# Two transformer layers on one core: layer 1's reciprocals per head and repeated by ScalarE, two pieces of layer 0 issued later

## The chip, the core and the metric

The kernel runs on one core of a Trainium2 chip. The core has TensorE (PE, matrix products; PEld is its weight load), VectorE (DVE), ScalarE (ACT), GpSimd (POOL) and SyncE (SP, here only an issuer of DMA transfers). Each engine works through its own queue in order and waits on semaphores for the others. The metric is the device time of one execution in microseconds; lower is better.

## The reference

Input is x of 2 sequences with 1024 tokens of 128 channels, all in float32. Two pre-norm layers are applied, each an attention and a mixture of experts, each added to x:

```python
x = x + _L0_attn_ref(_layernorm(x), ...)   # 16 heads of 64, with biases, no mask
x = x + _L0_ffn_ref(_layernorm(x), ...)    # 8 gated experts, top 2
x = x + _L1_attn_ref(_layernorm(x), ...)   # 16 heads of 8 plus 32 rotary dims, causal
x = x + _L1_ffn_ref(_layernorm(x), ...)    # a shared MLP and 8 experts, top 2
```

What matters for the change is in the two attentions. In layer 0, with s = 1/sqrt(64):

```python
q = z @ wq @ fcq_w + fcq_b;  k = z @ wk @ fck_w + fck_b
attn = softmax(q @ k.T * s);  out = attn @ v
```

In layer 1 each head has only 8 value channels, so a query tile's output is 16 heads x 8 channels = 128 rows, and each row is divided by its head's softmax sum.

## The kernel before

Tokens stand in tiles of 128. PSUM is split by three pools: ps_s (2 wide buffers for scores), ps_t (3 banks for transposes and everything small) and ps_a (1 accumulator). Inside `tc.manual_schedule` the instructions of TensorE, VectorE and ScalarE (in layer 1 GpSimd too) stand in the order in which the program issues them; elsewhere a scheduler places them. L404 and L415 are issued outside such a block, and the trace shows where they were put on VectorE: L404 between the statistics and L135, L415 between the normalisations.

*Start.* x is loaded by SP, then the three bias columns (L401, L404's input among them), while ScalarE issues the weight loads and GpSimd those of the router and the experts. L404 scales the query bias by s. `latents(0)` (L420) is the first layer norm (statistics L128 and L129, square root on ScalarE L134, reciprocal on VectorE L135, normalisation L153, transposes L147) and the projections to latents (L432, L433, L437). `project_qk` (L475) makes queries and keys of one pair of heads; ScalarE adds the biases (L488).

*Layer 0.* The loop at L600 runs over units (sequence b, pair of heads pr, query tile qt), 128 units. Three units are in flight: unit i gets scores (L501), row maximum (L510, VectorE) and exponentials (L520, ScalarE); unit i−1 gets its probabilities transposed (`fill`, L551) and moved out (`evict`, L557, one half by ScalarE, one by VectorE); unit i−2 gets its values (L568). When a pair is complete, at qt = 1 of the next pair, `reciprocals` (L523) inverts its softmax sums, 128x16, and `scale` (L528) transposes them on TensorE (L532), copies them out by ScalarE (L534), sends them by SP to DRAM (L538) and back, spread over partitions (L540, two transfers), and GpSimd multiplies the pair's output (L542). `project_qk` of the following pair stands in the units qt = 1 and 5. Side work fills other units: the layer norm of sequence 1 and the output weights while b = 0, `project_out` of sequence 0 at (1, 1), the router of sequence 0 from (1, 2). Layer 0's experts follow.

*Layer 1.* The loop at L1201 has the same shape, with causal lengths: scores L1078, masked maximum L1086, exponentials L1108, transposes L1120 with evictions L1126, values L1160. Units with qt < 4 are "short" and are issued two at a time. After the last unit of a query tile, `reciprocals` (L1129) inverts the softmax sums with each head's sum already repeated over its 8 channels: 128x128, and once more the first 64 columns (L1134, L1135). In the next unit `spread` (L1138) transposes the result (four matmuls, L1143), ScalarE copies it (L1145), and VectorE multiplies the tile's output (L1167). Sixteen query tiles end this way.

Of the kernel before, what the change touches and what calls it, by code (L numbers as in the profile page):

```python
# [11 lines left out]
F32 = mybir.dt.float32  # L12
# [3 lines left out]
ALU = mybir.AluOpType  # L16
# [3 lines left out]
P = 128  # L20
# [3 lines left out]
NT = T // P  # L24
# [5 lines left out]
H0, D0 = 16, 64  # L30
H1, D1, DR = 16, 8, 32
# [15 lines left out]
def bc(ap, shape):  # L47
    return ap.to_broadcast(list(shape))
# [3 lines left out]
def two_layers(ctx, tc, a, out):  # L52
    nc = tc.nc
# [9 lines left out]
    small = ctx.enter_context(tc.tile_pool(name="small", bufs=4))  # L63
# [4 lines left out]
    def bank():  # L68
        return psum["t"].tile([P, QB], F32, tag="t", name="ps_t")

    def acc_bank():
        return psum["a"].tile([P, QB], F32, tag="a", name="ps_a")

    def load(pool, name, shape, src, eng):
        t = pool.tile(list(shape), F32, tag=name, name=name)
        eng.dma_start(out=t if len(src.shape) == 2 else t.rearrange("p (a b) -> p a b", b=src.shape[-1])
                      if len(shape) == 2 else t, in_=src)
        return t
# [155 lines left out]
    def route0(b, pool, tag, bufs, got, gap):  # L234
        yield from layernorm_steps(b, pool, got, bufs, tag, gap=gap)
        yield
        yield from gates0(b, got)
# [149 lines left out]
    with ExitStack() as st:  # L387
# [11 lines left out]
        bias = {}  # L399
# [1 line left out]
            bias[k] = load(w0, f"b{k}", [P, NP], a[f"fc{k}"][D0:D0 + 1, :].rearrange("o (j p) -> p (o j)", p=P),  # L401
                           nc.sync)
        scaled_bq = w0.tile([P, NP], F32, tag="scaled_bq", name="scaled_bq")
        nc.vector.tensor_scalar(scaled_bq, bias["q"], 1.0 / math.sqrt(D0), None, ALU.mult)  # L404
        fco = load(w0, "fco", [P, NP, C], a["fco_w"].rearrange("(j p) c -> p j c", p=P), nc.scalar)
        fco_b = load(w0, "fco_b", [1, C], a["fco_b"], nc.scalar)

# [12 lines left out]
        def latents(b):  # L420

            got = []
            yield from layernorm_steps(b, a0, got, first=(b == 0))
            lnT = got[0]
            zqk = a0.tile([P, T], F32, tag="zqk", name="zqk", bufs=2)
            zv = a0.tile([P, NT, D0], F32, tag="zv", name="zv", bufs=2)
            lat[b] = zqk, zv
            for n in range(NQB):
                yield
                cols = slice(n * QB, (n + 1) * QB)  # L430
                ps = bank()
                nc.tensor.matmul(ps, wqk, lnT[:, cols], start=True, stop=True)  # L432
                nc.vector.tensor_copy(zqk[:, cols], ps)  # L433
            yield
            ps = bank()
            for t in range(NT):
                nc.tensor.matmul(ps[:, t * D0:(t + 1) * D0], lnT[:, t * P:(t + 1) * P], wv, start=True, stop=True)  # L437
            nc.scalar.copy(zv.rearrange("p t d -> p (t d)"), ps)
# [36 lines left out]
        def project_qk(b, pr, n):  # L475

            if n == 0:
                qk = a0.tile([P, 2, T], F32, tag="qk", name="qk", bufs=2)
                pairs[b, pr] = qk
            qk = pairs[b, pr]  # L480
            z, cols = lat[b][0], slice(n * QB, (n + 1) * QB)

            got = [acc_bank(), bank()]
            for h in range(2):
                rows = slice(h * D0, (h + 1) * D0)
                nc.tensor.matmul(got[h], fcqk[rows, pr * P:(pr + 1) * P], z[rows, cols], start=True, stop=True)  # L486
            for h, (scale, add) in enumerate(((1.0 / math.sqrt(D0), scaled_bq), (1.0, bias["k"]))):
                nc.scalar.activation(qk[:, h, cols], got[h], AF.Identity, bias=add[:, pr:pr + 1], scale=scale)  # L488
# [3 lines left out]
        probs, probsT, sums, recips, accs, aoTs = {}, {}, {}, {}, {}, {}  # L492
# [30 lines left out]
        def reciprocals(key):  # L523
            rs = small.tile([P, 2, NT], F32, tag="rs0", name="rs0", bufs=2)
            nc.vector.reciprocal(rs, sums.pop(key))
            return rs

        def scale(key, rs):  # L528

            b, pr = key  # L530
            ps = bank()
            nc.tensor.transpose(ps[:2 * NT, :P], rs.rearrange("p h t -> p (h t)"), ident)  # L532
            rows = small.tile([2 * NT, P], F32, tag="rsT0", name="rsT0", bufs=2)
            nc.scalar.copy(rows, ps[:2 * NT, :P])  # L534

            r = a0.tile([P, T], F32, tag="recip", name="recip", bufs=2)
            flat = dr.tile([2, T], F32, tag="flat", name="flat")
            nc.sync.dma_start(out=flat.rearrange("h (t p) -> (h t) p", p=P), in_=rows)  # L538
            for h in range(2):
                nc.sync.dma_start(out=r[h * D0:(h + 1) * D0, :], in_=bc(flat[h:h + 1, :], [D0, T]))  # L540
            o = aoTs[b][:, pr, :]
            nc.gpsimd.tensor_tensor(o, o, r, ALU.mult)  # L542
# [12 lines left out]
        def evict(i, h, ps, copy):  # L555
            for r in range(2):
                copy(probsT[i][h][:, :, r * 64:(r + 1) * 64], ps[r].rearrange("p (j q) -> p j q", q=64))  # L557
# [30 lines left out]
        with tc.manual_schedule(engines={ET.PE, ET.DVE, ET.Activation}):  # L588
            lat = {}
            for _ in latents(0):  # L590
                pass
            project_qk(0, 0, 0)
            project_qk(0, 0, 1)
            wout = w0.tile([P, NP, C], F32, tag="wout", name="wout")
            extra = [latents(1), output_weights()]
            routing = route0(0, f0w, "lnT", 1, routed0[0], 1)
            temp = [lambda: a0.tile([P, T], F32, tag="pT", name="h0", bufs=6)[:, :QB],
                    lambda: a0.tile([P, T], F32, tag="p", name="o0", bufs=4)[:, :QB]]
            experts = experts0(0, routed0[0], temp)
            for i in range(N + 3):  # L600
                s = scores(i) if i < N else None
                if 1 <= i <= N:
                    probsT[i - 1] = [a0.tile([P, NT, P], F32, tag="pT", name="pT", bufs=6) for _ in range(2)]
                    evict(i - 1, 0, fill(i - 1, 0), nc.scalar.copy)
                if i < N:
                    exponentials(i, [maximum(s[0]), maximum(s[1])])
                done = units[i - 2][:2] if i >= NT and i % NT == 1 else None
                if done:
                    rs = reciprocals(done)
                if 2 <= i <= N + 1:  # L610
                    values(i - 2)
                if 1 <= i <= N:
                    evict(i - 1, 1, fill(i - 1, 1), nc.vector.tensor_copy)
                    del probs[i - 1]
                if i >= N:
                    if i == N + 1:
                        scale(done, rs)
                        for t0 in (0, TPB):
                            project_out(NB - 1, t0, TPB, range(NP - 1))
                    experts(i < N + 2)  # L620
                    continue
                b, pr, qt = units[i]
                after = (b, pr + 1) if pr + 1 < NP else (b + 1, 0)
                if after[0] < NB and qt in (1, 5):
                    project_qk(*after, qt // TPB)
                if done:
                    scale(done, rs)
                if b == 0 and pr and qt not in (1, 5) and extra:
                    if next(extra[0], N) == N:
                        extra.pop(0)  # L630
                        if not extra:
                            obias = output_bias()
                            for bb in range(NB):
                                nc.gpsimd.tensor_tensor(xs[bb], xs[bb], bc(obias.unsqueeze(1), [P, NT, C]), ALU.add)
                if (b, pr) == (1, 1):
                    project_out(0, qt, 1, range(NP))
                if b == 1 and pr > 1 and qt not in (1, 5):
                    next(routing, None)
            for t0 in (0, TPB):
                project_out(NB - 1, t0, TPB, [NP - 1])  # L640
# [415 lines left out]
    with ExitStack():  # L1056
        units = [(b, qt, pr) for b in range(NB) for qt in range(NT) for pr in range(8)]
        N = len(units)
        probs, probsT, sums, recips, accs, outs = {}, {}, {}, {}, {}, {}
# [69 lines left out]
        def reciprocals(key):  # L1129


            full = small.tile([P, H1 + H1 // 2, D1], F32, tag="rsw1", name="rsw1", bufs=1)
            total = sums.pop(key)
            nc.vector.reciprocal(full[:, :H1, :], bc(total.unsqueeze(2), [P, H1, D1]))  # L1134
            nc.vector.reciprocal(full[:, H1:, :], bc(total[:, :H1 // 2].unsqueeze(2), [P, H1 // 2, D1]))  # L1135
            return full.rearrange("p h d -> p (h d)")

        def spread(key, full):  # L1138
# [40 lines left out]
        with tc.manual_schedule(engines={ET.PE, ET.DVE, ET.Activation, ET.Pool}):  # L1179
# [21 lines left out]
            for i in range(N + 3):  # L1201
# [45 lines left out]
                if i < N:  # L1247
                    b, qt, pr = units[i]
# [110 lines left out]
```

## Time and profile before

| | us |
|---|---|
| median of 3 runs | 1470.89 (1468.69 to 1470.93) |
| the profiled execution, its own time | 1473.5 |
| its span, first to last instruction | 1471.7 |
| PE busy | 1370.0 (93%) |
| DVE busy | 1045.8 (71%) |
| ACT busy | 903.9 (61%) |
| POOL busy | 271.0 (18%) |
| mean granted TensorE clock | 0.979 of full |

Stages by the timeline: start to 30 us, layer 0's attention to about 740, its experts to about 880, layer 1's attention to about 1360, then the rest of layer 1's experts. A timeline line gives the start in us, the length in us, engine, kernel line, operation, what it writes and reads, its shape and count, and in brackets how long the engine had stood idle and what ended that. A line of the chain gives start, length and what the chain passed through. A group's line ends with busy us, mean ns of one, and the idle time before. A line of the windows gives the stretch, its length, the busy time of the engine with its number of instructions, the granted clock, and the DMA share and rate.

### The profile page before, as it was taken

What the parts mean: (1) busy time and instruction counts of PE and PEld (TensorE: products, weight loads), DVE (VectorE), ACT (ScalarE), POOL (GpSimd) and SP (SyncE); (2) the same over time, 40 slices, a digit from 0 to 9 for tenths busy, and PEclk for the clock granted to TensorE, in tenths of its full rate; (3) what the DMA queues carried; (4) which work ended last, traced back from release to release, by engine and by line L of the source; (5) the groups of instructions that cost most, each with busy time, mean ns of one, the idle gap of its engine ahead of it and who ended that gap; (6) DMA issues with size and microseconds to landing.
All of it is one profiled execution on the core that took longest, in us unless ns stands there. A gap on an engine that the chain in (4) does not pass through costs nothing.

```text
span 1471.7 us, 40504 instructions
## 1 busy us (share of the span) xinstructions
PE 1370.0 (93%) x16930; PEld 977.9 (66%) x16930; DVE 1045.8 (71%) x2344; ACT 903.9 (61%) x1896; POOL 271.0 (18%) x246
## 2 busy tenths in 40 slices
PE   3999999999999999999998988999998899988997
PEld 1677777777777766777775555666665567766886
DVE  2787667777765877777745558767878867888776
ACT  2777666777755775777613336876756577764553
POOL 1000010000000100000053561102111031222673
PEclk9999999999999999999999979999978999999999
DMA  5000000000000000000010030000000011111463
GB/s 111 2 16 17 16 2 16 17 16 17 16 16 2 16 16 16 16 2 16 17 40 10 1 90 3 2 3 1 2 9 9 30 29 38 43 33 43 124 188 110
DMA packets 34391, 43.15 MB, mean 29 GB/s; under 512 B 10641, under 2 KB 22578, under 8 KB 34210
## 3 DMA queue, kind: packets, MB, share of 16 engines
q1 hardware_dynamic: 28288, 28.47, 7.1%
q0 software_dynamic: 4352, 10.70, 2.8%
q8 instruction: 134, 2.20, 0.6%
q10 hardware_dynamic: 1570, 1.41, 0.4%
q14 instruction: 47, 0.39, 0.1%
HBM read 35.51 MB, written 5.05 MB: 28 GB/s over the span
## 4 chain that ended last, share of the span: by engine, by line
PE 71%; DVE 16%; ACT 5%; issue 5%; DMA 2%; POOL 0%; SPq 0%; DVEq 0%; POOLq 0%; ACTq 0%
PE ps_s L501 15%; PE ps_a L568 13%; PE ps_s L1078 8%; PE ps_t L551 8%; PE ps_t L1120 4%; PE ps_s L253 3%; PE ps_a L1160 3%; DVE p L510 3%; PE ps_a L486 2%; DVE ps_s L1086 2%; PE ps_t L583 2%; ACT p L1108 2%; PE ps_t L954 2%; PE ps_t L946 2%; PE ps_t L714 2%
## 5 line engine op out<-in xcount | busy, mean ns | idle before, releaser
L510 DVE CUSTOM_DVE_ANT_0 p<-ps_s,zero 128x1024 f32<-128x1024 f32 x256 | 303.4, 1222 | 136.9 <-PE ps_s L501 136.0
L520 ACT ACTIVATE p<-p,nmx 128x1024 f32<-128x1024 f32 x256 | 293.1, 1153 | 4.9 <-DVE nmx L510 4.8
L557 ACT COPY pT<-ps_t 128x512 f32<-128x512 f32 x256 | 137.5, 589 | 196.5 <-PE ps_t L551 196.5
L501 PE MATMUL ps_s<-qk 64*128 64x512 f32 x1024 | 254.5, 611 | 3.4 <-DVE nmx L510 2.9
L568 PE MATMUL ps_a<-pT,zv 128*64 128x128 f32 x4096 | 251.9, 276 | 0.0
L568 PEld LDWEIGHTS ps_a<-pT,zv 128*64 128x64 f32 x4096 | 220.9, 137 | 9.4 <-issue 0.8
L551 PEld LDWEIGHTS ps_t<-ident,p 64*128 64x128 f32 x4096 | 159.7, 139 | 90.9 <-issue 83.3
L557 DVE COPY pT<-ps_t 128x512 f32<-128x512 f32 x256 | 164.7, 685 | 53.8 <-PE ps_t L551 53.8
L1078 PE MATMUL ps_s<-k,qm 64*128 64x512 f32 (+3 forms) x768 | 173.7, 541 | 15.8 <-ACT p L1108 11.2
L551 PE MATMUL ps_t<-ident,p 64*128 64x64 f32 x4096 | 177.4, 226 | 1.3 <-DVE pT L557 0.7
L1086 DVE CUSTOM_DVE_ANT_0 p<-ps_s,cmask 128x640 f32<-128x640 f32 (+3 forms) x128 | 125.9, 1021 | 64.8 <-PE ps_s L1078 57.5
L542 POOL TENSOR_TENSOR aoT<-aoT,recip 128x1024 f32<-128x1024 f32 x16 | 37.9, 2368 | 641.0 <-DMA recip<-flat 536.1
L501 PEld LDWEIGHTS ps_s<-qk 64*128 64x128 f32 x1024 | 91.0, 188 | 81.1 <-issue 69.1
L1120 PEld LDWEIGHTS ps_t<-ident,p 64*128 64x128 f32 x2304 | 104.8, 143 | 47.3 <-issue 23.1
L1126 ACT COPY pT<-ps_t 128x512 f32<-128x512 f32 (+3 forms) x192 | 95.9, 535 | 63.9 <-PE ps_t L1120 62.8
L1108 ACT ACTIVATE p<-p,nmx 128x640 f32<-128x640 f32 (+3 forms) x128 | 125.9, 992 | 4.3 <-DVE nmx L1086 4.2
L1078 PEld LDWEIGHTS ps_s<-k,qm 64*128 64x128 f32 x768 | 73.4, 198 | 82.4 <-issue 40.6
L1120 PE MATMUL ps_t<-ident,p 64*128 64x64 f32 x2304 | 118.3, 231 | 2.4 <-ACT pT L1126 1.3
L1160 PE MATMUL ps_a<-pT,vx 128*32 128x128 f32 x2304 | 100.7, 283 | 7.2 <-DVE pT L1126 7.1
L1126 DVE COPY pT<-ps_t 128x128 f32<-128x128 f32 (+3 forms) x192 | 87.2, 482 | 3.3 <-PE ps_t L1120 2.6
L1108 ACT ACTIVATE p<-ps_s,nmx 128x128 f32<-128x128 f32 (+3 forms) x128 | 66.5, 526 | 26.7 <-DVE nmx L1086 26.4
L1086 DVE CUSTOM_DVE_ANT_0 ps_s<-ps_s,cmask 128x128 f32<-128x128 f32 (+3 forms) x128 | 63.6, 498 | 25.4 <-PE ps_s L1078 22.1
(248 smaller groups left out, 1779.0 us busy)
## 6 DMA issues: line engine op xcount, KB each, us to landing
we<-in_we SPq DMA_DIRECT2D x52, 256.0 KB, 2.8
recip<-flat SPq DMA_DIRECT2D x32, 256.0 KB, 4.0
we<-in_we POOLq DMA_DIRECT2D x1, 2048.0 KB
z<-results SPq DMA_DIRECT2D x6, 256.0 KB, 4.7
x<-in_x SPq DMA_DIRECT2D x4, 256.0 KB, 6.0
up<-in_up_proj POOLq DMA_DIRECT2D x1, 1024.0 KB, 12.7
normed<-y SPq DMA_DIRECT2D x3, 256.0 KB, 2.3
out_x<-x SPq DMA_DIRECT2D x3, 256.0 KB, 2.8
```

Of the source, the lines that this page charges most:

```text
L501: nc.tensor.matmul(s[h][:, n * QB:(n + 1) * QB], qk[rows, 0, qt * P:(qt + 1) * P], qk[rows, 1, n * QB:(n + 1) * QB], start=True, stop=True)
L510: nc.vector.tensor_tensor_reduce(p, s, bc(zero, [P, T]), -1.0, 3e38, ALU.add, ALU.min, nmx)
L520: nc.scalar.activation(p, p, AF.Exp, bias=nmx, scale=-1.0, accum_out=ssum[:, h, qt:qt + 1])
L551: nc.tensor.transpose(ps[r][:, k * 64:(k + 1) * 64], probs[i][h][rows, k * P:(k + 1) * P], ident[rows, rows])
L557: copy(probsT[i][h][:, :, r * 64:(r + 1) * 64], ps[r].rearrange("p (j q) -> p j q", q=64))
L568: nc.tensor.matmul(acc[h * D0:(h + 1) * D0, cols], zv[:, j, :], probsT[i][h][:, j, :], start=(j == 0), stop=(j == NT - 1))
L1078: nc.tensor.matmul(s[h][:, n * QB:n * QB + w], qms[b, qt][rows, pr, :], kTs[b][pr // 4][rows, n * QB:n * QB + w], start=True, stop=True)
L1086: nc.vector.tensor_tensor_reduce(to[:, :nk], s[:, :nk], cmask[:, T - nk:], -1.0, 3e38, ALU.add, ALU.min, nmx)
L1108: nc.scalar.activation(p[:, h, :nk], s[h][:, :nk], AF.Exp, bias=nmx[h], scale=-1.0, accum_out=sums[b, qt][:, head:head + 1])
L1120: nc.tensor.transpose(ps[r][:, c * 64:(c + 1) * 64], probs[i][rows, h, j * P:(j + 1) * P], ident[rows, rows])
L1126: copy(probsT[i][:, 8 * f:8 * f + n, r * 64:(r + 1) * 64], ps[r][:, :n * 64].rearrange("p (j q) -> p j q", q=64))
L1160: nc.tensor.matmul(acc[to * 32:(to + 1) * 32, k * P:(k + 1) * P], vx[:, j, g, pr % 4 * 24:pr % 4 * 24 + 32], probsT[i][:, h * (qt + 1) + j ...
```

## The change

Three things are altered. The scaling of the query bias is issued by VectorE after `latents(0)`, inside the hand-ordered block, instead of ahead of it. In layer 0's loop `scale` is called in the unit qt = 3 instead of qt = 1; `reciprocals` stays at qt = 1, and the tail call after the last pair is as before. In layer 1 VectorE takes the reciprocal of the 16 sums once, and ScalarE writes the repeated forms with two broadcast copies.

```diff
@@ -401,7 +401,6 @@
         scaled_bq = w0.tile([P, NP], F32, tag="scaled_bq", name="scaled_bq")
-        nc.vector.tensor_scalar(scaled_bq, bias["q"], 1.0 / math.sqrt(D0), None, ALU.mult)
         fco = load(w0, "fco", [P, NP, C], a["fco_w"].rearrange("(j p) c -> p j c", p=P), nc.scalar)
@@ -589,6 +588,7 @@
             for _ in latents(0):
                 pass
+            nc.vector.tensor_scalar(scaled_bq, bias["q"], 1.0 / math.sqrt(D0), None, ALU.mult)
             project_qk(0, 0, 0)
             project_qk(0, 0, 1)
@@ -606,7 +606,7 @@
                 done = units[i - 2][:2] if i >= NT and i % NT == 1 else None
                 if done:
-                    rs = reciprocals(done)
+                    rs = done, reciprocals(done)
@@ -614,7 +614,7 @@
                     if i == N + 1:
-                        scale(done, rs)
+                        scale(*rs)
@@ -623,8 +623,8 @@
                     project_qk(*after, qt // TPB)
-                if done:
-                    scale(done, rs)
+                if i >= NT and qt == 3:
+                    scale(*rs)
                 if b == 0 and pr and qt not in (1, 5) and extra:
@@ -1129,10 +1129,11 @@
         def reciprocals(key):
+            rs = small.tile([P, H1], F32, tag="rs1", name="rs1", bufs=1)
+            nc.vector.reciprocal(rs, sums.pop(key))
             full = small.tile([P, H1 + H1 // 2, D1], F32, tag="rsw1", name="rsw1", bufs=1)
-            total = sums.pop(key)
-            nc.vector.reciprocal(full[:, :H1, :], bc(total.unsqueeze(2), [P, H1, D1]))
-            nc.vector.reciprocal(full[:, H1:, :], bc(total[:, :H1 // 2].unsqueeze(2), [P, H1 // 2, D1]))
+            nc.scalar.copy(full[:, :H1, :], bc(rs.unsqueeze(2), [P, H1, D1]))
+            nc.scalar.copy(full[:, H1:, :], bc(rs[:, :H1 // 2].unsqueeze(2), [P, H1 // 2, D1]))
             return full.rearrange("p h d -> p (h d)")
```

## The prediction

> **What bounds the kernel now.** The change touches three places far apart, so I read each place for itself, starting with the list of who waited for whom and the chain that ended last. At the start of the kernel both name the same transfer. First the list (waiter, releaser, us in total, times, longest), then the chain over the first 40 us (start, length, what):
>
> ```profile
> DVE scaled_bq L404 <- DMA bq<-in_fcq: 11.5, 1, 11.5
> ```
>
> ```profile
> 3.76 15.09 DMA bq<-in_fcq
> 18.85 0.02 issue
> 18.87 0.17 DVE scaled_bq L404
> 19.04 0.12 DVE rstd L135
> ```
>
> VectorE stands 11.47 us before the bias scaling, and behind it in its queue stands L135, the reciprocal of the standard deviation, without which nothing of the first layer norm can go on. The timeline says how long L135 had been ready, and what comes later:
>
> ```profile
> 11.82 0.30 ACT L134 ACTIVATE rstd<-bnmv,eps_col 128x8 f32<-128x8 f32 x1
> 18.87 0.17 DVE L404 TENSOR_SCALAR scaled_bq<-bq 128x8 f32<-128x8 f32 x1 [11.47 <-DMA bq<-in_fcq]
> 18.95 0.20 DVE L135 RECIPROCAL rstd<-rstd 128x8 f32<-128x8 f32 x1
> 25.47 0.69 DVE L433 COPY zqk<-ps_t 128x512 f32<-128x512 f32 x1 [0.98 <-PE ps_t L432]
> 28.25 0.69 ACT L488 ACTIVATE qk<-ps_a,scaled_bq 128x512 f32<-128x512 f32 x1 [0.47 <-PE ps_t L486]
> 28.84 0.68 ACT L488 ACTIVATE qk<-ps_t,bk 128x512 f32<-128x512 f32 x1
> ```
>
> From about 30 us TensorE is the bound (page: PE 1370.0 us busy, 93%). In layer 0's attention a unit takes 4.81 us, and TensorE hardly pauses. The start of each unit is the first score product, L501; here are units qt=1 to qt=7 of pair 7, and then qt=1 and 2 of the last pair, which projects no next pair:
>
> ```profile
> 336.96 1.93 PE L501 MATMUL ps_s<-qk 64*128 64x512 f32 x8
> 343.45 1.99 PE L501 MATMUL ps_s<-qk 64*128 64x512 f32 x8
> 348.31 1.94 PE L501 MATMUL ps_s<-qk 64*128 64x512 f32 x8
> 353.12 1.93 PE L501 MATMUL ps_s<-qk 64*128 64x512 f32 x8
> 357.92 1.93 PE L501 MATMUL ps_s<-qk 64*128 64x512 f32 x8
> 364.01 1.88 PE L501 MATMUL ps_s<-qk 64*128 64x512 f32 x8
> 368.76 1.51 PE L501 MATMUL ps_s<-qk 64*128 64x512 f32 x6
> ...
> 694.67 1.93 PE L501 MATMUL ps_s<-qk 64*128 64x512 f32 x8
> 699.78 1.99 PE L501 MATMUL ps_s<-qk 64*128 64x512 f32 x8
> 704.63 1.94 PE L501 MATMUL ps_s<-qk 64*128 64x512 f32 x8
> ```
>
> qt=1 and qt=2 take 6.49 + 4.86 us; qt=5 and qt=6, with the same projection but no scale(), take 6.09 + 4.75. In layer 1 a tile of queries ends 16 times; where units are short, TensorE waits there for the reciprocals (the worst of the 16):
>
> ```profile
> 1145.88 0.94 DVE L1134 RECIPROCAL rsw<-ssum 128x128 f32<-128x128 f32 x1
> 1146.74 0.49 DVE L1135 RECIPROCAL rsw<-ssum 128x64 f32<-128x64 f32 x1
> 1146.87 0.90 PE L1143 MATMUL ps_t<-ident,rsw 128*128 128x128 f32 x4 [1.96 <-DVE rsw L1134]
> ```
>
> **Part A, the bias scaling.** L404 moves behind the latents on VectorE. L135 can then start when ScalarE's square root ends, 11.82 + 0.30 = 12.12, plus some 0.06 for the handover: 12.2 instead of 18.95, so 6.75 us earlier. Does the chain keep this until 30 us? The moved instruction follows the second L433, which ends at 26.16 − 6.75 = 19.4; bq landed at 18.85, so it no longer waits, and its own 0.17 us lie under TensorE's projection. Its user L488 comes at 28.25 − 6.75 = 21.5. The other late transfer is bk, issued at 4.17 and 15.9 us in landing: 20.1, against its use at 28.84 − 6.75 = 22.1, a cover of 2.0 us. The fcqk halves land by 10.7, wv by 4.9. Unknown is rank, the input of L415 on VectorE: it is issued on GpSimd's queue after router (landed 5.4) and before up (landed 15.9), and its own landing is not shown. L415 sits between the normalisations, at about 13 in the new order; if rank came with up it would cost up to 2.9 us, with router nothing. By size (32 KB against up's 1024 KB) I take nothing. ScalarE was idle 8.25 us there, its DMA issues are over at 10.5 and stay the gate. **A = −6.7 us, between −3.8 and −6.8.**
>
> **Part B, scale() at qt=3 instead of qt=1.** It happens 15 times; the reciprocal itself (0.25 us of VectorE) stays at qt=1. It moves one transpose, L532 (0.28 us), one ScalarE copy, L534 (0.24 us), three SP transfers and GpSimd's product L542 (2.37 us). Leaving qt=1 saves (6.49 + 4.86) − (6.09 + 4.75) = 0.51 us, less about 0.1 because the reciprocal still pushes the aoT copy that L486 waits for: 0.4, in 14 pairs. At qt=3 the price is nearest to the last pair's row, where scale() stands without a projection: 699.78 − 694.67 + 704.63 − 699.78 − 2 × 4.81 = 0.34; with VectorE free of the reciprocal and the aoT copy I take 0.3 (floor 0.2, L532's own share of TensorE). Net −0.1 × 14 = −1.4. Against it: scale() now takes the third of the three ps_t banks just ahead of the side work of the same unit. Five pairs have side work with a bank at qt=3 (layer norm steps, output weights, project_out, gates). That work then needs the bank whose eviction, L557 on VectorE (0.69 us), has only begun, some 0.4 us of TensorE idle each: +2.0. The GpSimd product ends about 10.5 us after L532, so now two units (9.6 us) later; the next GpSimd work in its queue, the power of the side layer norms at 109.96 and 511.76, comes still 4 to 6 us behind it, and pair 7's rows are needed by project_out only a pair later. SP carries nothing else here. **B = +0.5, between −3.5 and +4** (the ends: bank waits nought; twice as long and the 0.34 in full).
>
> **Part C, reciprocals once per head.** VectorE: 0.94 + 0.49 give way to one of 128x16. L525 is such a row: 0.25. ScalarE gains two copies SBUF to SBUF. The nearest rows from PSUM are the 128x128 forms of L966 (255 ns) and L1126 (265 ns). [...] I take 0.30 + 0.24, overlapped by 0.09 as back-to-back rows are: 0.45. Where ScalarE is idle, the second half of the spread is ready 0.25 + 0.06 + 0.45 + 0.05 = 0.8 us after the reciprocal begins, instead of 1.4: 0.6 sooner. [...]
>
> Now the 16 ends. Five wait for VectorE (from 882.5, 897.6, 917.4, 1120.1, 1145.9): 3 × 0.6, 0.55 and 0.5 (there L1078 caps it) = −2.8. The end at 1075.4 gives −0.2. At 939.4 and 1174.9 ScalarE is just done with its copy (940.39 and 1175.84), so the new copies end as late as the old reciprocals: 0. At 968.5 the exponentials end at 970.12, the copies at 970.57, and L1143, which ran at 970.15, waits: +0.3. At the other seven L1143 begins over 0.3 us after ScalarE's exponentials, or TensorE is held by something else: 0, hidden behind score products. The 1.2 us that VectorE saves each time is also hidden; without that cover it would be 19 us. **C = −2.7, between −5 and +1.**
>
> **Sum.** −6.7 + 0.5 − 2.7 = −8.9. The profiled execution took 1473.5 us (span 1471.7), so it would take 1464.6; the runs' median is 2.6 lower, 1470.89 − 8.9 = **1462.0**. Within 0.2% (2.9 us) a measurement can't tell a change from none.
>
> **The rivals.**
> 1. *A new wait at the start* (rank, or bk if it lands later than shown): A falls to −3.8 or less. For it: GpSimd's queue hides rank's landing; against it: the sizes. Time 1465 to 1468.
> 2. *The moved scale() isn't neutral.* All bank waits hidden gives 1458; twice the waits gives 1465.5. The last pair's 0.34 is the only direct row.
> 3. *ScalarE's copies hold up the spread at the long ends too*: they come behind four exponentials. At 10 ends up to 0.45 each would turn C into +1.8: 1466.5. Against it is the slack counted above.
> 4. *Slower: the granted clock.* The windows of the trace show stretches where the clock falls to half:
>
> ```profile
> 1080.00:1100.00 20.00, 17.59 (x118) 0.67 0.05 15
> ```
>
> [...] The mean is 0.979: (1 − 0.979) × 1471.7 / 0.5 = 62 us at half. [...] Each further us at half costs about 0.45 us where TensorE is the bound; 26 us more would use up the gain and leave the same time, 33 us more (mean below 0.968) makes it slower: 1474 and up. Fewer such windows would give 1455.
>
> **How the numbers follow.** The reading above 0.60 (its own range 1459 to 1465); rival 1 0.10; rival 2 beyond that 0.12, half to each side; rival 3 0.07; the clock 0.11, of which 0.04 faster still, 0.04 around the old time, 0.03 slower. Range 1456 to 1467.5 leaves out about 2 in 10. Faster 0.90, same 0.07, slower 0.03.
>
> **What would show it.** A: L135 at 12.2, the first L501 at 23.2 instead of 29.95, no wait for bq. B: qt=1 of pair 7 at 6.1 to 6.2 us, qt=3 and 4 together 9.9. C: the copies at 0.3 and 0.24 us, L1143's wait at the five ends shorter by 0.5. The prediction is wrong if the first L501 lies after 26 us, or the layer 0 pairs grow, or the mean clock moves by over 0.01.

## The result and the profile after

The changed kernel takes 1464.44 us (median of 6 runs, 1461.44 to 1465.46); the kernel before, run beside it, 1471.07 (6 runs, 1468.69 to 1471.94). The ratio is 0.9954, with a 95% interval of 0.9941 to 0.9966: 6.6 us or 0.46% faster. The forecast was 1462.0 with a range of 1456 to 1467.5. The profiled execution of the changed kernel took 1464.07 us (span 1462.3, granted clock 0.982), against 1473.5 (1471.7, 0.979) before. So the two traces differ by 9.4 us and the medians by 6.6; where that gap may come from is taken up below.

The first view is the chain that ended last in the changed kernel, over the start (start, length, what it passed through). Line numbers between 405 and 590 are one lower than before: L501 is now L500, L534 is L533.

```profile
1.78 8.44 DMA x<-in_x
10.22 0.02 issue
10.24 0.49 ACTq L76
10.73 0.03 issue
10.76 1.28 ACT L134
```

The transfer of `bq`, 15.09 us of the old chain, is gone from it. The piece before the square root is now ScalarE's own queue: its last DMA issue ends at 10.73, then comes the loading of its table. The chain puts the landing of a piece of x ahead of that issue; the square root itself needs only the statistics, and VectorE has finished them at 7.40 us. Whether the queue or x holds it is tested below (`a_act_free`). The timeline of the same stretch:

```profile
12.06 0.30 ACT L134 ACTIVATE rstd<-bnmv,eps_col 128x8 f32<-128x8 f32 x1
12.39 0.20 DVE L135 RECIPROCAL rstd<-rstd 128x8 f32<-128x8 f32 x1 [4.99 <-ACT rstd L134]
19.57 0.16 DVE L591 TENSOR_SCALAR scaled_bq<-bq 128x8 f32<-128x8 f32 x1
22.02 0.69 ACT L487 ACTIVATE qk<-ps_a,scaled_bq 128x512 f32<-128x512 f32 x1 [0.47 <-PE ps_t L485]
22.61 0.68 ACT L487 ACTIVATE qk<-ps_t,bk 128x512 f32<-128x512 f32 x1
23.72 0.59 PE L500 MATMUL ps_s<-qk 64*128 64x512 f32 x2
```

L135 starts at 12.39 instead of 18.95. The moved bias scaling, now L591, has no bracket: it waits for nothing, but by only 0.2 us, as `bq`, issued at 3.76, landed 15.6 us later. The first score product starts at 23.72 instead of 29.95, 6.23 us sooner. Of these only 5.05 are left when pair 1 begins, because pair 0 then contains 6.8 us of TensorE's clock at half speed instead of 3.4. In the windows (stretch, length, TensorE busy and its instructions, granted clock, DMA share and rate) the first line is before's, the other two are after's:

```profile
20.00:40.00 20.00, 16.65 (x71) 0.91 0.00 0
```

```profile
20.00:40.00 20.00, 16.69 (x117) 0.83 0.01 1
1080.00:1100.00 20.00, 15.64 (x136) 0.83 0.05 15
```

From 20 to 40 us the clock is lower after (0.83 for 0.91), from 1080 to 1100 it is higher (0.83 for the 0.67 shown of before). In slices of 1 us over the whole of both traces the granted clock reads 1.00 or 0.50, and something between only in slices where it changes. So what it lacks of full speed, doubled and times the length, is the time at half speed. Over the whole span it comes to 53.7 us instead of 60.7.

In layer 0 these are the score products that open the units qt=1 to qt=6 of pair 7:

```profile
333.27 1.94 PE L500 MATMUL ps_s<-qk 64*128 64x512 f32 x8
339.45 1.88 PE L500 MATMUL ps_s<-qk 64*128 64x512 f32 x8
344.21 1.94 PE L500 MATMUL ps_s<-qk 64*128 64x512 f32 x8
349.31 1.99 PE L500 MATMUL ps_s<-qk 64*128 64x512 f32 x8
354.17 1.94 PE L500 MATMUL ps_s<-qk 64*128 64x512 f32 x8
360.26 1.88 PE L500 MATMUL ps_s<-qk 64*128 64x512 f32 x8
```

qt=1 takes 6.18 (6.49 before), qt=2 4.76, qt=3 5.10 (4.81 before), qt=4 4.86. A pair without side work takes 41.36 us instead of 41.41. Two kinds of pair do not look like that, and neither was priced rightly. Four pairs with side work grow: pair 2 from 44.59 to 45.29, pair 3 from 50.22 to 51.07, pair (1,1) from 58.20 to 59.16, pair (1,3) from 45.77 to 46.47. And one pair, (1,4), shrinks from 46.36 to 44.20. Here is the extra time of pair 2 in the timeline:

```profile
129.19 0.28 PE L531 MATMUL ps_t<-ident,rs 128*16 128x128 f32 x1
129.29 1.29 DVE L556 COPY pT<-ps_t 128x512 f32<-128x512 f32 x2 [0.55 <-PE ps_t L550]
129.89 0.20 ACT L519 ACTIVATION_READ_ACCUMULATOR p<-p,nmx 128x1 f32 x1
129.98 0.24 ACT L533 COPY rsT<-ps_t 16x128 f32<-16x128 f32 x1
...
130.27 0.44 PE L147 MATMUL ps_t<-ident,lny 128*128 128x128 f32 x2 [0.80 <-ACT rsT L533]
```

TensorE does the transpose of the reciprocals at 129.19, and then stands 0.80 us until ScalarE has copied it out, before the side work (L147) gets its bank. The wait occurs four times, at 130.27, 178.37, 439.35 and 534.65, with 0.80 or 0.81 us each.

In layer 1, the worst end of a query tile (1146.87 before):

```profile
1136.21 0.24 DVE L1133 RECIPROCAL rs<-ssum 128x16 f32<-128x16 f32 x1
1136.48 0.30 ACT L1135 COPY rsw<-rs 128x128 f32<-128x128 f32 x1 [2.04 <-DVE rs L1133]
1136.68 0.24 ACT L1136 COPY rsw<-rs 128x64 f32<-128x64 f32 x1
...
1136.83 0.71 PE L1144 MATMUL ps_t<-ident,rsw 128*128 128x128 f32 x4 [1.58 <-ACT rsw L1135]
```

From the start of the reciprocal to the first spread product are 0.62 us; before it was 0.99 (1145.88 to 1146.87). The whole stay of the four spread products, wait and run, shrinks from 2.86 to 2.29 us.

By stages the traces differ as follows (after minus before): up to the first score product −6.23; pair 0 +1.18 (the clock); pairs 1 to 14 +0.64; the last pair and layer 0's experts nothing; layer 1's attention, first to last score product, 473.07 to 468.81 = −4.26; the rest −0.8.

### The profile page after: what moved, and what is told of

Read it like the earlier page. It is cut to its first block, busy times and chain, and to the rows that moved or that the text cites. A ratio compares the mean times of both kernels' runs of the same rounds, so it can differ in the third digit from the quotient of the medians.

```text
span 1462.3 us, 40488 instructions
## 1 busy us (share of the span) xinstructions
PE 1365.6 (93%) x16930; PEld 979.6 (67%) x16930; DVE 1027.6 (70%) x2328; ACT 909.3 (62%) x1928; POOL 271.5 (19%) x246
## 3 DMA queue, kind: packets, MB, share of 16 engines
HBM read 35.51 MB, written 5.05 MB: 28 GB/s over the span
## 4 chain that ended last, share of the span: by engine, by line
PE 73%; DVE 14%; ACT 7%; issue 5%; DMA 1%; POOL 0%; DVEq 0%; ACTq 0%; SPq 0%; POOLq 0%
PE ps_s L500 16%; PE ps_a L567 12%; PE ps_s L1078 8%; PE ps_t L550 8%; PE ps_t L1120 4%; PE ps_a L1161 3%; PE ps_s L253 3%; DVE p L509 3%; PE ps_a L485 2%; DVE ps_s L1086 2%; PE ps_t L954 2%; PE ps_t L946 2%; ACT p L1108 2%; PE ps_t L582 2%; PE ps_t L714 2%
## 5 line engine op out<-in xcount | busy, mean ns | idle before, releaser
L500 PE MATMUL ps_s<-qk 64*128 64x512 f32 x1024 | 253.3, 609 | 2.0 <-DVE nmx L509 1.4
L500 PEld LDWEIGHTS ps_s<-qk 64*128 64x128 f32 x1024 | 92.9, 189 | 84.8 <-issue 74.5
L1126 ACT COPY pT<-ps_t 128x512 f32<-128x512 f32 (+3 forms) x192 | 95.9, 534 | 62.5 <-PE ps_t L1120 61.1
L1126 DVE COPY pT<-ps_t 128x128 f32<-128x128 f32 (+3 forms) x192 | 87.3, 482 | 3.8 <-PE ps_t L1120 3.1
```

Of the source, the lines that this page charges most:

```text
L500: nc.tensor.matmul(s[h][:, n * QB:(n + 1) * QB], qk[rows, 0, qt * P:(qt + 1) * P], qk[rows, 1, n * QB:(n + 1) * QB], start=True, stop=True)
L1126: copy(probsT[i][:, 8 * f:8 * f + n, r * 64:(r + 1) * 64], ps[r][:, :n * 64].rearrange("p (j q) -> p j q", q=64))
```

## The experiments

They ran on three chips. On the first the kernel before takes 1470.73 us (51 runs, 1463.84 to 1475.78), on the second 1504.51 (11 runs), on the third 1503.03 (11 runs). So only ratios to the kernel before on the same chip are compared. One per mille is 1.5 us.

The theory was the prediction's: A gives nearly all, by the early L135; B is about neutral, with gains at qt=1 eaten by waits for a bank; C gives what five ends of a query tile save. The rivals were that the moved `scale` loses what C gives, that C gives nothing by itself, and that the clock makes the difference.

**Each part alone, and the change without B** (first chip). `a_only` has just this:

```diff
-        nc.vector.tensor_scalar(scaled_bq, bias["q"], 1.0 / math.sqrt(D0), None, ALU.mult)
...
             for _ in latents(0):
                 pass
+            nc.vector.tensor_scalar(scaled_bq, bias["q"], 1.0 / math.sqrt(D0), None, ALU.mult)
```

> Only the query bias's scaling is moved behind the latents. Theory (three parts that add up: the start gives nearly all of the gain): first score product at 23.7 us instead of 29.95, as in the changed kernel, and 5 to 6 us faster (1465 to 1466), because up to 1 us of the 6.2 goes back to a longer stretch of half clock at about 30 us. Rival (the gain at the start is taken back by later transfers, layer 1 gives the rest): less than 3 us faster.

Measured: 1465.27, ratio 0.9960 (0.9948 to 0.9972), so −5.9 us. The reciprocal L135 starts at 10.51 and the first score product at 20.62.

`b_only` moves just the call of `scale`:

```diff
-                if done:
-                    scale(done, rs)
+                if i >= NT and qt == 3:
+                    scale(*rs)
```

> Only scale() is moved to qt = 3. Theory: plain pairs gain 0.05 us each; the four units with side work after scale() lose 0.8 us each to the wait for ScalarE's copy of the rows (3.2 us), pair 4 of sequence 1 gains about 2 us because GpSimd's product no longer falls on the router's small VectorE steps; sum -0.5 to +1 us, not to be told from no change. Rival (the move is what saves): 2 us faster or more.

Measured: 1472.69, ratio 1.0009 (0.9998 to 1.0020), +1.3 us. The four waits of 0.8 us are there, and pair (1,4) takes 44.16 us.

`c_only` changes layer 1's `reciprocals` alone:

```diff
-            nc.vector.reciprocal(full[:, :H1, :], bc(total.unsqueeze(2), [P, H1, D1]))
-            nc.vector.reciprocal(full[:, H1:, :], bc(total[:, :H1 // 2].unsqueeze(2), [P, H1 // 2, D1]))
...
+            nc.vector.reciprocal(rs, sums.pop(key))
...
+            nc.scalar.copy(full[:, :H1, :], bc(rs.unsqueeze(2), [P, H1, D1]))
+            nc.scalar.copy(full[:, H1:, :], bc(rs[:, :H1 // 2].unsqueeze(2), [P, H1 // 2, D1]))
```

> Only layer 1's reciprocals are changed. Theory: five of 16 query tiles end 0.5 to 0.6 us sooner, the eleven others within 0.1 us: 1 to 3 us faster. Rival (the copies hold up the spread at the long tiles, or the stretch of half clock moves): the same time or slower, with waits of L1143 over 0.3 us at long tiles.

Measured: 1469.01, ratio 0.9994 (0.9984 to 1.0004), −0.9 us by the ratio and not told from nothing. The wait at the worst end is 1.59 us, as in the whole change (1.58), for 1.96 before.

`a_and_c` is the whole change with `scale` left at qt = 1.

> The change without the move of scale(). Theory: the parts add up, 7 to 8 us faster than before, so equal to the whole change or up to 1 us better. Rival (the move of scale() saves something): slower than the whole change by 1 us or more.

Measured: 1461.95, ratio 0.9943 (0.9923 to 0.9963), −8.4 us. Against `a_only` it is 3.3 us faster by the medians (2.5 by the ratios), so C is worth between 0.9 (alone) and 3.3 us (on top of A). Against the whole change (0.9954) it is about 1.6 us better, which agrees with B's +1.3: the part that moves `scale` costs rather than gives. Neither of these two differences clears its interval alone; they agree in sign.

**Why do side-work units wait?** In `scale_after_scores` (second chip) the whole change stands, but `scale` is called in qt = 4, straight after that unit's score products:

```diff
                 s = scores(i) if i < N else None
+                if NT <= i < N and units[i][2] == 4:
+                    scale(*rs)
...
-                if i >= NT and qt == 3:
-                    scale(*rs)
```

> The whole change, but scale() is issued at qt = 4 right behind that unit's score products, so that side work of the unit before no longer stands behind it in TensorE's queue. Theory (side work waited for ScalarE's copy of the rows, which stands behind the exponentials): the four waits of 0.8 us vanish, plain pairs take 41.2 to 41.4 us, pair 4 of sequence 1 stays near 44.2 us; 3 to 4 us faster than the whole change, so about 10 us faster than before. Rival (the wait only moves to the transposes behind the scores): equal to the whole change.

Measured: 1489.37, ratio 0.9909 (0.9892 to 0.9927). All four waits are gone: the side-work pairs take 44.57, 50.19, 58.43 and 45.74 us. Plain pairs stay at 41.37, because L532's transpose costs its 0.36 us in qt = 4 as well. So nothing is hidden there; only the wait for the bank is avoided.

Which engine does the bank wait for? The prediction named an eviction on VectorE, while the trace of after names ScalarE's copy of the rows. In `rows_by_dve` (third chip, a single run, 1487.0) VectorE makes that copy:

```diff
-            nc.scalar.copy(rows, ps[:2 * NT, :P])
+            nc.vector.tensor_copy(rows, ps[:2 * NT, :P])
```

> The whole change with VectorE instead of ScalarE copying the 16 rows out of scale()'s bank; VectorE comes to it after both evictions. Theory (side work behind scale() waits for that copy): its four waits grow from 0.8 to about 1.3 us, and the releaser is VectorE's copy. Rival (side work waits for the eviction L557, as the prediction had it): the waits stay at 0.8 us or shrink to 0.4.

The timeline of this kernel at the same place:

```profile
124.33 0.28 PE L531 MATMUL ps_t<-ident,rs 128*16 128x128 f32 x1
124.43 1.29 DVE L556 COPY pT<-ps_t 128x512 f32<-128x512 f32 x2 [0.55 <-PE ps_t L550]
...
125.17 0.44 PE L147 MATMUL ps_t<-ident,lny 128*128 128x128 f32 x2 [0.57 <-DVE pT L556]
...
125.63 0.27 DVE L533 COPY rsT<-ps_t 16x128 f32<-16x128 f32 x1
```

The waits shrank to 0.57 us at all four places instead of growing to 1.3, so the theory above fell. L147 starts 0.57 us after the transpose ends, released by the eviction, and 0.46 us before the rows are copied at all. If the rows' copy itself were what side work must wait for, L147 could not have started before 125.90. So it waits for whichever bank it is handed: in the changed kernel the one that ScalarE frees (0.80 us), here the one that VectorE's eviction frees (0.57 us), as the prediction had it. Why the handed bank differs was not settled.

**Why does pair (1,4) shrink?** In the trace of before, the timeline shows VectorE's router work of sequence 0 beside GpSimd's product of the pair:

```profile
580.94 0.23 DVE L189 TENSOR_TENSOR r_eq<-r_pr,r_m 128x64 f32<-128x64 f32 x1
...
581.31 2.36 POOL L542 TENSOR_TENSOR aoT<-aoT,recip 128x1024 f32<-128x1024 f32 x1 [43.64 <-DVE r_eq L189]
581.46 0.22 DVE L191 TENSOR_REDUCE r_k<-r_eq 128x8 f32<-128x64 f32 x1
581.72 2.03 DVE L192 TENSOR_TENSOR r_h<-r_eq,r_k 128x64 f32<-128x64 f32 x1
583.67 1.21 DVE L510 CUSTOM_DVE_ANT_0 p<-ps_s,zero 128x1024 f32<-128x1024 f32 x1
...
584.94 1.12 PE L501 MATMUL ps_s<-qk 64*128 64x512 f32 x2 [1.43 <-DVE nmx L510]
```

L192 takes 2.03 us instead of some 0.23, and ends just after L542 ends (583.67). L510, the row maximum of the unit, stands behind it, and the next score product on TensorE (L501) waits 1.43 us for that maximum. L191 ran beside the same product in its usual 0.22; it reads one operand from SBUF, L192 two, but no run shows that this makes the difference. To test it, `one_pair` is the kernel before with `scale` later in this pair only (second chip, a single run):

```diff
-                if done:
-                    scale(done, rs)
+                if i >= NT and qt == (3 if (b, pr) == (1, 4) else 1):
+                    scale(*rs)
```

> The kernel before, with scale() at qt = 3 in pair 4 of sequence 1 alone. Theory (there GpSimd's product falls on the router's small VectorE steps and the two hold each other up): the step r_h L192 takes 0.22 us instead of 2.03, and the pair 44.2 us instead of 46.4. Rival (the gain of that pair comes from the moved transposes): the step stays at about 2 us, or the pair over 46 us.

```profile
578.02 0.22 DVE L191 TENSOR_REDUCE r_k<-r_eq 128x8 f32<-128x64 f32 x1
578.27 0.23 DVE L192 TENSOR_TENSOR r_h<-r_eq,r_k 128x64 f32<-128x64 f32 x1
578.42 1.22 DVE L510 CUSTOM_DVE_ANT_0 p<-ps_s,zero 128x1024 f32<-128x1024 f32 x1
```

With GpSimd's product out of the way L192 takes 0.23 us. The wait of TensorE for L510 is gone too. The pair itself took 42.50 us, but there its first unit also ran in 4.86 us instead of 6.50, because no half-speed stretch fell on it. Without its first unit the pair takes 39.86 us in before and 37.64 in both the changed kernel and `one_pair`. The whole run took 1495.34. In the five traces that keep `scale` at qt = 1, one of L190 and L192 takes 2.0 to 2.3 us beside the product; in the eight that move it in this pair, none does.

**What gates the start now?** The new chain shows ScalarE's queue: its DMA issues stand before the table load and the square root. `a_act_free` (A and C, second chip) moves three weight loads from ScalarE's queue to SP's, behind the biases:

```diff
-        fco = load(w0, "fco", [P, NP, C], a["fco_w"].rearrange("(j p) c -> p j c", p=P), nc.scalar)
+        fco = load(w0, "fco", [P, NP, C], a["fco_w"].rearrange("(j p) c -> p j c", p=P), nc.sync)
```

(`fcv` and `fco_b` likewise.) The doubt was whether the key bias, which had landed at 19.5 us, would then be the gate.

> The change without the move of scale(), and three weight loads (fcv, fco, fco_b) go from ScalarE's queue to SP's, behind the bias columns. Theory (after the move the start is set by ScalarE's DMA issues, with the key bias right behind): the table load begins before 5 us, the reciprocal L135 runs at 7.8 us, but the first score product at 20.3 us or later, because the bias of the keys lands at about 19.4 us; 0 to 1.5 us faster than without this. Rival (ScalarE's issues alone set the start): first score product at 18.5 us, 3 us faster.

```profile
2.99 1.28 ACT L134 ACT_TABLE_LOAD   x1 [2.99 <-issue]
7.27 0.30 ACT L134 ACTIVATE rstd<-bnmv,eps_col 128x8 f32<-128x8 f32 x1 [2.99 <-DVE bnmv L129]
7.60 0.20 DVE L135 RECIPROCAL rstd<-rstd 128x8 f32<-128x8 f32 x1 [0.37 <-ACT rstd L134]
15.60 0.17 DVE L590 TENSOR_SCALAR scaled_bq<-bq 128x8 f32<-128x8 f32 x1 [1.36 <-DMA bq<-in_fcq]
```

Measured: 1485.37, ratio 0.9892 (0.9873 to 0.9911), first score product at 18.03. The table load waits no longer for the queue, the square root waits for its statistics, and L135 starts at 7.60. So both had stood behind those issues and needed no landing of x; what spaces the issues themselves is not shown. My theory that the key bias would gate the start at 19.4 was wrong: the instruction that adds it (L486) runs at 17.05 without waiting, while in the five traces of the old load order that show its landing it came at 19.3 to 20.1. In this kernel `fcv` and `fco` are issued only at 10.65 and 14.61 us, behind the biases; whether that makes the key bias land earlier is not shown. VectorE waits 1.36 us for `bq`, without holding up TensorE.

`bias_rows` adds to this `scale` after the scores, and loads the three biases as 24 rows of 512 bytes, which TensorE transposes (the loads are not shown):

```diff
+            ps = bank()
+            nc.tensor.transpose(ps[:, :3 * NP], brows, ident[:3 * NP, :3 * NP])
+            nc.vector.tensor_scalar(scaled_bq, ps[:, :NP], 1.0 / math.sqrt(D0), None, ALU.mult)
+            nc.vector.tensor_copy(bcols, ps[:, NP:3 * NP])
```

> scale() behind the scores at qt = 4, the three loads on SP, and the biases loaded as 24 rows of 512 bytes and transposed on TensorE instead of as single elements. Theory (nothing but the two gates above holds the start): first score product at 18 to 19 us, about 13 us faster than before, and no wait for a bias. Rival (another load or a longer stretch of half clock takes their place): first score product after 20.5 us, no faster than scale() behind the scores alone.

Measured: 1485.61, ratio 0.9887 (0.9868 to 0.9906), first score product at 18.88. The rows bring nothing: the start is no earlier than without them (18.03 in `a_act_free`), where the biases' landing had stopped being the gate. Beside `scale_after_scores` on the same chip, from which it differs in its loads (these three moved, the biases as rows), it is 3.8 us faster by the medians.

**The best version.** `all_three` (third chip) is the whole change with `scale` after the scores at qt = 4 and the three loads on SP's queue, with the biases as they were; `after_again` is the whole change, beside it on the same chip.

> The whole change once more, as a yardstick on the chip of the two runs beside it: 0.4 to 0.6% faster than before.

> The whole change with scale() behind the scores at qt = 4 and the three loads on SP, the biases loaded as before. Theory (the start's gate is the reciprocal L135 and nothing behind it; the four waits are gone; no small VectorE step meets GpSimd's product): first score product at 18 to 18.5 us, 12 to 16 us faster than before and 5 us or more faster than the whole change. Rival (gains at the start are lost to half clock or to a later load): within 2 us of the whole change.

Measured: `after_again` 1493.88, ratio 0.9937 (0.9915 to 0.9958), in line with 0.9954 on the first occasion. `all_three` 1482.62, ratio 0.9869 (0.9847 to 0.9891): 11.3 us below the whole change. Its start:

```profile
7.36 0.30 ACT L134 ACTIVATE rstd<-bnmv,eps_col 128x8 f32<-128x8 f32 x1 [3.08 <-DVE bnmv L129]
7.70 0.20 DVE L135 RECIPROCAL rstd<-rstd 128x8 f32<-128x8 f32 x1 [0.37 <-ACT rstd L134]
...
17.49 1.02 PE L499 MATMUL ps_s<-qk 64*128 64x512 f32 x4
```

The first score product is 5.6 us earlier than in `after_again` (23.10), and pairs 1 to 14 are 4.3 us shorter (614.75 for 619.03). Of these 4.3, the four waits make 3.1; the other 1.3 stand in pair (1,4), on which a half-speed stretch falls in the trace of `after_again` alone. But `after_again` had a late start among the six traces of the new order with ScalarE's loads as before. Their first score products come at 20.34 to 23.72 us, 21.98 in the mean, and those of the three kernels with the loads moved at 17.49, 18.03 and 18.88, 18.13 in the mean. So the moved loads are worth about 3.9 us at the start, as in `bias_rows`, and with the four waits 7 of the 11.3 us are accounted for. The rest was not followed up.

## Why the prediction was right, point by point

The direction, the size and the order of the parts held: A carries the change, C is small, B about nil to slightly negative. The forecast of −8.9 us met −9.4 between the two traces and −6.6 between the medians. That the traces come so near is in part luck: of A's 6.7 us only 5.05 were left at pair 1, and layer 1 and its tail gave 5.0 instead of 2.7, with 13 us less at half speed in layer 1's attention.

*A, −6.7 predicted.* The mechanism held: no wait for `bq`, L135 at 12.39 (12.2 predicted), first score product at 23.72 (23.2 predicted). `rank` and `bk` made no wait, so rival 1 fell. But as a gain over the typical execution A was mis-sized. The term was read from one trace and then taken off the median: "the runs' median is 2.6 lower, 1470.89 − 8.9". In the old order L135 follows the landing of `bq`, which varies from execution to execution, and that trace had the latest of the four. In the new order it follows the last DMA issue on ScalarE's queue, which varies too. L135 starts (us, traces of several chips):

| order | traces | mean |
|---|---|---|
| before's | 18.95, 17.55, 14.70, 15.93 | 16.8 |
| after's, ScalarE's loads as before | 12.39, 10.51, 10.17, 11.45, 12.66, 10.29 | 11.2 |

The difference of the means is 5.5 us, and `a_only` gave 5.9. Between the first rows of the two lines it is 6.6, and that is what the trace comparison saw. It goes far to explain why the before trace was itself 2.4 us slower than its median (1473.5 for 1471.07): its L135 was 2.2 us later than the mean. That the medians follow these starts is argued from ten traces, not shown for each run. The clock is a rival for the same gap: the trace of after had 7.0 us less at half speed, and in pair 0 3.4 us more of it cost 1.18 us, so an estimate by that rate gives 2.4 us. The two were not separated.

*B, +0.5 predicted.* Measured +0.64 over the pairs of the trace and +1.3 (−0.3 to +2.9) alone, so the sum was near, but by two misses that cancel. (Its lower end of −3.5 does not come out of its terms: without the bank waits they give −1.4. And "the layer 0 pairs grow", one of its own signs of being wrong, came true for four pairs and for the sum, as B = +0.5 itself implied.) "Five pairs have side work with a bank at qt=3 ... some 0.4 us of TensorE idle each: +2.0" was right in its kind and wrong in its size: four pairs with a wait of 0.8 us, grown by 0.7 to 0.96 each, +3.2. This is the branch of rival 2 with twice the waits. The fifth, (1,4), shows no such wait. In the plain pairs −0.05 each came instead of −0.1: qt=1 saves 0.31, qt=2 0.1, qt=3 and qt=4 cost 0.35. And −2.2 us in pair (1,4) were not foreseen at all: the text weighed what GpSimd's product would delay on its own queue, not what it blocks on VectorE. The traces show that: L192 took 2.03 us beside a 2.36 us product in before, and 0.23 in the changed kernel and in `one_pair`, where the product comes later. Why the product holds it up was not shown.

*C, −2.7 predicted.* The 0.30 and 0.24 of the forecast come from no row of before and no run; in their place the changed kernel showed 0.297 and 0.245 us for the two copies (medians of 16). The rows of before lay further off for 128x128: 0.255 and 0.265 out of PSUM (L966, L1126), and 0.399 for L937, out of SBUF with a scale column (means). The stays of the spread products at the five ends, wait and run, fell from 1.72 to 1.22, 1.26 to 0.74, 2.21 to 1.65, 1.23 to 0.71 and 2.86 to 2.29, that is by 0.50, 0.52, 0.56, 0.52 and 0.57. The end that was to lose 0.3 (968.5) lost 0.13. Rival 3, copies held up at ten long ends, fell: of the others, apart from the first of sequence 1, where the clock differed, none changed by over 0.1. Layer 1's attention took 468.81, 469.42 and 469.57 us in the traces of after, `c_only` and `a_and_c`, and 473.07, 472.18 and 471.87 in those of before, `a_only` and `b_only`: 3.1 less by the means. The time at half speed within it is 34.1, 36.6 and 37.5 us in the first three and 47.3, 44.4 and 34.1 in the others. The whole change and `b_only` have the same 34.1, and they too differ by 3.1 us (468.81 and 471.87), so the amount at half speed does not make the difference. Where the stretches fall can still matter: in sequence 1, before and after differ by 2.0 us in each of two stretches between ends in which after has less of it. In sequence 0, up to its last end, the whole change gained 0.8 us and `c_only` 1.2, although the stays there shrink by 1.5 together and the prediction's share was 1.7.

*The sum.* With A at its measured −5.9, B at +1.3 and C between −0.9 and −3.3, the parts give −5.5 to −7.9, and the whole change −6.6. *The clock* (rival 4) moved by 0.003 in the mean, towards faster, within the bound of 0.01 that the prediction had set for itself. (Its 0.45 us for each us at half speed was the author's estimate, which no run tested; pair 0 gave 1.18 us for 3.4, or 0.35. At 0.45, 20 us more would have used up the 8.9, not 26; nothing hung on it.)

## What to carry to other kernels

Where an instruction's end is set by a transfer, one trace shows one landing (here L135, behind `bq`, started at 14.70 to 18.95 us in four traces): take several traces, or a mean, before the gain is set against a median. A wait that is removed shows the next gate; here it was ScalarE, held by its own DMA issues, and moving three loads off its queue brought the start forward by another 3.9 us in the mean. Where work is moved past other engines' work, look also at what it blocks while it runs (here L192 on VectorE, 2.03 us for 0.23), not only at what it is waited for, and at who needs the buffer that it takes.

## What the runs showed of the hardware that was not expected

The landing of `bq`, 1024 numbers issued at 3.6 to 3.8 us in each trace, came between about 14.6 and 18.9 us in the old order, in executions of the same start, and at 14.1 and 19.4 in two traces of the new order. So this small load took 10.5 to 15.6 us, with large loads in flight beside it; that these cause it is not shown.

The first table load on ScalarE began behind the DMA issues that stand before it in the same queue: between 8.54 and 11.03 us in ten traces, and at 3.0 in the three in which three of the issues were on SP's queue.

A VectorE operation on 128x64 numbers grew from 0.23 to between 2.0 and 2.3 us when its two operands in SBUF met a GpSimd product of 2.36 us; a VectorE reduction with one SBUF operand beside the same product kept its 0.22.

TensorE's half-speed stretches fell at other places in each trace, for 49.8 to 60.7 us in all in six of them (before, after and the four of the first chip) and for 64.3 to 92.2 in the other seven, and these runs show no rule for it.
